# A four-layer image kernel on one core: some depthwise-convolution taps of the head moved from TensorE to VectorE

## The chip, the core and the metric

The kernel runs on one core of one Trainium2 chip. It uses TensorE for matrix products into PSUM (the memory that products accumulate in), VectorE, ScalarE and GpSimd for elementwise work, and SyncE to issue nearly all DMAs. In the profile these engines are PE (PEld for its weight loads), DVE, ACT, POOL and SP. [...] The metric is the device time of one execution in microseconds; a time given for a kernel is the median over several executions.

## The reference, cut to what matters

The input is four images of 96 channels and 64 x 64 pixels. Four layers are added to it in turn, each on a group-normalised copy of what came before.

```python
# layer 0: attention, plus a depthwise 5x5 convolution of v ("positional")
lepe = lax.conv_general_dilated(v, lepe_w, (1, 1), [(2, 2), (2, 2)], feature_group_count=C) + lepe_b
out = proj_w @ (feature + lepe) + proj_b
x = x + out
# layer 1: a state-space block; its input goes through a depthwise 3x3 convolution first
xz = jnp.einsum('bchw,oc->bohw', gn(x), in_proj_w)
xi, z = jnp.split(xz, 2, axis=1)                      # 192 channels each
xi = silu(conv2d(xi, conv_w, conv_b, groups=192, pad=1))
...                                                   # four directional scans over xi, then more convolutions
```

A depthwise convolution multiplies, for each channel, 25 (or 9) shifted copies of the image by one number each and adds them up. Layers 2 and 3 have convolutions and a second state-space block of the same kind.

## The kernel before, in words

**Stages.** `first(b)` computes layer 0 and the input half of layer 1 for image b; `second(b)` and `third(b)` the rest. The long recurrences of the two state-space blocks (the scans) are cut into 3072 units. The program has three parts. The head is `first(0)` alone, with `solo[0]` true. Then comes the scan part: 3072 calls of `unit`, with the stages of the other images laid beside them. Last comes the tail, `third` of the last image, again with `solo[0]` true. The scan part is emitted under a manual schedule, that is, in the order in which the program writes it. In the head the scheduler of the language orders the instructions of each engine.

**A convolution on TensorE.** Channels lie on the partitions. `diagonals` (from L1070) makes for each tap a 96 x 96 matrix that has that tap's 96 channel weights on its diagonal; `conv` (from L1083) multiplies it with the shifted window of a padded image and accumulates over the taps in one PSUM bank. One product covers 8 rows of 64 pixels, 512 columns; an image takes eight such chunks. In the profile one fp32 product shows as two matmul records.

**Positional convolution** (in `first`, from L1326). The padded image `vpad` is 68 x 68. For each of eight chunks j: 25 products into a bank, then VectorE adds the bank and the bias to `feat` (L1342), TensorE multiplies `feat` by the projection (l0_proj), VectorE adds that to `xn` (L1348), and the result is stored. After all eight, a group norm.

**Input convolution** (`in_conv`, from L1097). For each half h of 96 channels: eight products fill the padded image `upad` (66 x 66), copied in by ScalarE (L1107); then for each of eight chunks 9 products, a Silu from PSUM to `ur` by ScalarE (L1114), a transposed copy `uc` by ScalarE (L1115) and a store of `ur` (L1116). The transposed image is stored at the end of the half. `in_conv` is also called later, in `first` and `second` of other images, while scans run; there `solo[0]` is false.

**Banks in the head.** `bank()` with `solo[0]` true hands out halves of a two-bank tile `bx`, and two such tiles exist; so two convolutions share a tile, and the next two share the other. The waits follow the whole tile: the second convolution of a tile waits for the Silu that reads the first half.

**After the head.** `prepare(0)` makes the inputs of the first scan group from stored `ur` pieces (tile `us`, L1698): two small products per half, copies to `pr` (L1720), stores and loads, several ScalarE and GpSimd steps. Then `fetch`, `decays`, `drive`, `times_b` and the first `scan` (L1836) follow.

Of the kernel before, what the change touches and what calls it, by code (L numbers as in the profile page):

```python
# [9 lines left out]
F32 = mybir.dt.float32  # L10
BF16 = mybir.dt.bfloat16
AF = mybir.ActivationFunctionType
ALU = mybir.AluOpType
# [4 lines left out]
B, C, H, W = 4, 96, 64, 64  # L18
# [11 lines left out]
PCH = 512  # L30
# [162 lines left out]
def _view(t, slot, rows=None):  # L193
    n, m, shape = slot
    v = t[: rows or t.shape[0], n : n + m]
    if len(shape) == 1:
        return v
    names = "abcd"[: len(shape)]
    return v.rearrange(f"p ({' '.join(names)}) -> p {' '.join(names)}",
                       **{k: s for k, s in zip(names, shape)})  # L200
# [693 lines left out]
def streams(ctx: ExitStack, tc: tile.TileContext, x, wts, cst, out, wat, cat, flag):  # L894
# [3 lines left out]
    nc = tc.nc  # L898
# [16 lines left out]
    def wv(name, rows=None):  # L915
        return _view(wt, wat[name], rows)
# [27 lines left out]
    def img(t):  # L944
        return t.rearrange("p (a b) -> p a b", b=W)

    def mm(o, lhsT, rhs, first=True, last=True):
        nc.tensor.matmul(o, lhsT=lhsT, rhs=rhs, start=first, stop=last)  # L948

    solo = [True]  # L950
    spare = []

    def bank():
        if solo[0]:
            if not spare:
                t = ps.tile([128, CH], F32, tag="bx", name="bx")
                spare.extend((t[:, PCH:], t[:, :PCH]))
            return spare.pop()
        return ps.tile([128, PCH], F32, tag="one", name="one")
# [5 lines left out]
    def border(pad, k):  # L965
        n = pad.shape[1]
        for s in (pad[:, 0:k, :], pad[:, n - k : n, :], pad[:, k : n - k, 0:k], pad[:, k : n - k, n - k : n]):
            nc.gpsimd.memset(s, 0.0)
# [38 lines left out]
    with tc.tile_pool(name="start", bufs=1) as T:  # L1007
        t0 = T.tile([128, cst.shape[1] - n2], F32, name="t0")
        nc.scalar.dma_start(out=t0, in_=cst[:, n2:])
        n, m, shape = wat["l1_alog"]  # L1010
# [4 lines left out]
        n, m, shape = cat["spread"]  # L1015
        nc.vector.tensor_copy(spread, t0[:, n - n2 : n - n2 + m])
        for tag in ("l1_", "l3_"):
            decay[tag] = keep.tile([128, 4, E // 8], F32, name=tag + "decay")
            n, m, shape = cat[tag + "alogn"]
            src = _view(t0, (n - n2, m, shape))  # L1020
            if tag == "l3_":
                nc.scalar.activation(decay[tag], src, AF.Exp)
                src = decay[tag]
# [46 lines left out]
    def diagonals(pool, w, name="diag"):  # L1070

        taps = w.shape[1]
        w = w[:, :taps]
        d = pool.tile([96, taps, 96], F32, tag=name, name=name, bufs=1)
        nc.gpsimd.tensor_tensor(  # L1075
            d,
            ident[:96, :96].unsqueeze(1).to_broadcast([96, taps, 96]),
            w.unsqueeze(2).to_broadcast([96, taps, 96]),
            ALU.mult,
        )  # L1080
        return d

    def conv(o, weight, src, j, k=3):  # L1083


        n = k * k
        taps = [(weight[:, t, :], src[:, 8 * j + t // k : 8 * j + t // k + 8, t % k : t % k + W]) for t in range(n)]
        for t, (lhsT, rhs) in enumerate(taps):
            mm(o, lhsT, rhs, t == 0, t == len(taps) - 1)
            if t < len(taps) - 1:  # L1090
                yield (1,)
        yield

    def inner(pad, j):
        return pad[:, 1 + 8 * j : 9 + 8 * j, 1 : 1 + W]

    def in_conv(pool, tag, b, w, src):  # L1097

        pad = pool.tile([96, PADW, PADW], F32, name="upad", bufs=1)
        border(pad, 1)  # L1100
        for h in range(2):
            dg = diagonals(pool, wv(tag + "conv")[:, h, :])
            for j in range(8):
                p = bank()
                mm(p[:96], w[:, bass.ts(h, 96)], src[:, bass.ts(j, PCH)])
                yield
                nc.scalar.copy(inner(pad, j), img(p[:96]))  # L1107
                yield 1
            uc = pool.tile([96, W, H], F32, name="uc", bufs=1)
            for j in range(8):  # L1110
                p = bank()
                yield from conv(p[:96], dg, pad, j)
                ur = pool.tile([96, PCH], F32, name="ur", bufs=2)
                nc.scalar.activation(ur, p[:96], AF.Silu, bias=wv(tag + "conv_b")[:, h : h + 1])  # L1114
                nc.scalar.copy(uc[:, :, 8 * j : 8 * j + 8], ur.rearrange("p (a b) -> p b a", b=W))  # L1115
                nc.sync.dma_start(out=u_row[h][b][:, bass.ts(j, PCH)], in_=ur)  # L1116
                yield 1
            for j in range(4):
                nc.sync.dma_start(out=u_col[h][b][:, bass.ts(j, CH)],
                                  in_=uc.rearrange("p a b -> p (a b)")[:, bass.ts(j, CH)])  # L1120
# [179 lines left out]
    def first(b):  # L1300

        with tc.tile_pool(name="p1", bufs=1) as P:
            xn = P.tile([96, L], F32, name="xn")
            for j in range(4):
                nc.sync.dma_start(out=xn[:, bass.ts(j, CH)], in_=x[b][:, bass.ts(j, CH)])
            yield from group_norm(xn, img(xn))
            with tc.tile_pool(name="p1d", bufs=1) as D:
                samp = D.tile([96, 34, 34], F32, name="samp")
                dist = D.tile([96, 34, 34], F32, name="dist")
                for t in (samp, dist):  # L1310
                    border(t, 1)
                with tc.tile_pool(name="p1t", bufs=2) as T:
                    xv = xn.rearrange("p (i r j s) -> p i r j s", r=2, j=W // 2, s=2)
                    t0 = T.tile([96, 32, 32], F32, tag="t", name="t0")
                    t1 = T.tile([96, 32, 32], F32, tag="t", name="t1")
                    nc.vector.tensor_add(t0, xv[:, :, 0, :, 0], xv[:, :, 0, :, 1])
                    nc.vector.tensor_add(t1, xv[:, :, 1, :, 0], xv[:, :, 1, :, 1])
                    nc.vector.tensor_add(t0, t0, t1)
                    nc.vector.tensor_scalar(samp[:, 1:33, 1:33], t0, 0.25, None, ALU.mult)
                yield 2  # L1320
                yield from attention(b, xn, samp, dist)
                with tc.tile_pool(name="p1f", bufs=1) as FP:
                    feat = FP.tile([96, L], F32, name="feat")
                    yield from neighbours(b, xn, samp, dist, feat)
                    with tc.tile_pool(name="l0c", bufs=1) as pool:
                        w = staged(pool, "l0_v", "l0_proj")  # L1326
                        vpad = pool.tile([96, 68, 68], F32, name="vpad")
                        border(vpad, 2)
                        dg = diagonals(pool, wv("l0_lepe"))
                        for j in range(8):  # L1330
                            p = bank()
                            mm(p[:96], w["l0_v"], xn[:, bass.ts(j, PCH)])
                            yield
                            nc.scalar.copy(vpad[:, 2 + 8 * j : 10 + 8 * j, 2 : 2 + W], img(p[:96]))
                            yield 1
                        for j in range(4):
                            nc.sync.dma_start(out=xn[:, bass.ts(j, CH)], in_=x[b][:, bass.ts(j, CH)])
                        for j in range(8):
                            js = bass.ts(j, PCH)
                            p = bank()  # L1340
                            yield from conv(p[:96], dg, vpad, j, 5)
                            nc.vector.scalar_tensor_tensor(out=feat[:, js], in0=p[:96], scalar=wv("l0_lepe_b"),  # L1342
                                                           in1=feat[:, js], op0=ALU.add, op1=ALU.add)
                            yield 1
                            q = bank()
                            mm(q[:96], w["l0_proj"], feat[:, js])
                            yield
                            nc.vector.scalar_tensor_tensor(out=xn[:, js], in0=q[:96], scalar=wv("l0_proj_b"),  # L1348
                                                           in1=xn[:, js], op0=ALU.add, op1=ALU.add)
                            nc.sync.dma_start(out=res1[b][:, js], in_=xn[:, js])  # L1350
                            yield 1
            yield from group_norm(xn, img(xn))
            for j in range(4):
                nc.sync.dma_start(out=gate1[b][:, bass.ts(j, CH)], in_=xn[:, bass.ts(j, CH)])
            with tc.tile_pool(name="p1i", bufs=1) as pool:
                w = staged(pool, "l1_in")["l1_in"]
                yield from in_conv(pool, "l1_", b, w, xn)
# [615 lines left out]
    def beside(s):  # L1973
        stages = {"first": first, "second": second, "third": third}
        for n, b in BESIDE[s]:
            yield from stages[n](b)
# [50 lines left out]
    p = bank()  # L2027
# [36 lines left out]
```

## Time and profile before

| what | value |
|---|---|
| median of three executions | 15068.81 us (15060.3 to 15096.54) |
| the profiled execution, its own time | 15038.64 us |
| its span | 15036.8 us |
| busy over the span: PE, DVE, ACT, POOL | 82%, 78%, 55%, 69% |
| granted TensorE clock, mean | 0.809 |
| positional convolution of the head | 456 to 635 us |
| input convolution of the head | 642 to 786 us |
| first scan starts | 830.41 us |

How to read the profile: times are counted from the start of the span. A group's row gives the line, engine, operation, out<-in with shapes, its count, then busy time and the mean length of one, and then how long the engine sat idle just before and what released it. In a table by stretches each engine has its busy time and, in brackets, the number of instructions; behind them stand the granted TensorE clock (1.00 is full speed), the mean busy share of the 16 DMA engines, and GB/s. In a timeline a row gives start, length, engine, line, operation and count; in square brackets stands the idle time before it. The profiled execution is one of several, and it is 30 us below the median of the others.

### The profile page before, as it was taken

The page shows a single profiled execution, that of the slowest core. Times are in us where ns is not written, and L with a number is a line of the kernel's source. Part 1 is how long each engine was busy: PE and PEld are TensorE (multiplying, and loading weights), DVE is VectorE, ACT ScalarE, POOL GpSimd, SP SyncE. Part 2 cuts the span into 40 slices and gives each one's busy share as a digit, 9 for nine tenths or more (in the row PEclk, how much of TensorE's full clock was granted, in tenths as well). Part 3 has the DMA queues.
Part 4 walks back from the last instruction along what each step waited for, and adds up shares of the span by engine and source line. Part 5 has one row for each costly group of instructions (what it writes and reads, how often), then busy time and mean ns, then how long its engine had stood idle before and what let it go on. Part 6 is the DMA issues. An engine that isn't in the chain of part 4 may idle for free. (4 is left out here: it accounts for less than half of the span.)

```text
span 15036.8 us, 127166 instructions
## 1 busy us (share of the span) xinstructions
PE 12260.5 (82%) x40658; PEld 3344.2 (22%) x40658; DVE 11679.2 (78%) x7517; ACT 8280.8 (55%) x11648; POOL 10375.2 (69%) x4746
## 2 busy tenths in 40 slices
PE   8978886888969787889868887897969888667757
PEld 2322221222212222222212221221212222111111
DVE  0067888888878888778887798798878888777784
ACT  3155555555745566555655556455755567545652
POOL 0056787777868777668776787786777778666672
PEclk9978886898969888789867797797879888667666
DMA  0066788786878778667876788687877868666682
GB/s 9 26 149 163 177 202 213 175 211 171 215 178 203 195 183 209 167 168 197 208 179 158 170 204 222 174 203 180 203 195 192 203 173 221 168 166 167 167 204 68
DMA packets 902136, 2644.32 MB, mean 176 GB/s; under 512 B 107280, under 2 KB 257392, under 8 KB 901456
## 3 DMA queue, kind: packets, MB, share of 16 engines
q1 hardware_dynamic: 900800, 2634.83, 71.0%
q8 instruction: 323, 5.29, 0.2%
q14 instruction: 357, 2.92, 0.1%
q10 hardware_dynamic: 656, 1.27, 0.0%
HBM read 2169.08 MB, written 466.62 MB: 175 GB/s over the span
## 5 line engine op out<-in xcount | busy, mean ns | idle before, releaser
L1848 POOL TENSOR_TENSOR rep<-hs,bc 128x1024 f32<-128x1024 f32 x3072 | 7230.5, 2358 | 3160.0 <-DVE hs L1836 2682.5
L1836 DVE TENSOR_TENSOR_SCAN hs<-rep,carry,bx 128x1024 f32<-128x1024 f32 x2304 | 5401.4, 2344 | 277.9 <-POOL rep L1848 15.0
L1829 DVE TENSOR_TENSOR bx<-bx,bc 128x1024 f32<-128x1024 f32 x3072 | 3720.1, 1211 | 1033.6 <-PE bx L948 998.6
L1815 ACT ACTIVATE rep<-rep,l_decay 128x1024 f32<-128x1024 f32 x3072 | 3495.9, 1143 | 903.6 <-DMA rep<-dd 883.7
L948 PE MATMUL bx<-parts,spread 24*128 24x512 bf16 x6144 | 1413.5, 438 | 1812.0 <-DVE hs L1836 1762.5
L948 PE MATMUL acc<-rep,ct 128*32 128x512 f32 x12288 | 2603.0, 732 | 184.9 <-POOL rep L1848 184.9
L1836 DVE TENSOR_TENSOR_SCAN hs<-rep,bx 128x1024 f32<-128x1024 f32 x768 | 1754.2, 2284 | 306.9 <-POOL rep L1848 224.9
L948 PEld LDWEIGHTS <-spread 24*128 24x128 bf16 x6144 | 310.1, 93 | 4297.8 <-DVE hs L1836 2925.5
L948 PE MATMUL one<-band,dg 96*96 96x512 f32 x2304 | 1117.9, 621 | 0.0
L948 PE MATMUL one<-upad,diag 96*96 96x512 f32 x2016 | 1021.0, 643 | 3.2 <-ACT ur L1114 2.7
L948 PEld LDWEIGHTS acc<-rep,ct 128*32 128x32 f32 x12288 | 507.5, 126 | 1958.9 <-issue 1482.0
L948 PE MATMUL one<-qq,kk 96*128 96x512 f32 x1152 | 820.7, 802 | 133.8 <-ACT ex L1234 80.1
L1234 ACT ACTIVATE ex<-one 128x512 f32<-128x512 f32 x576 | 342.8, 595 | 754.1 <-PE one L948 749.3
L948 PE MATMUL one<-pr,ct 6*96 6x512 f32 x1024 | 647.1, 732 | 29.7 <-ACT pr L1720 4.1
L1815 ACT ACT_TABLE_LOAD x470 | 603.0, 1283 | 116.4 <-DMA rep<-dd 108.7
L948 PE MATMUL one<-hp,diag 96*96 96x512 f32 x1152 | 606.5, 665 | 48.0 <-POOL diag L1075 48.0
L948 PE MATMUL one<-vpad,diag 96*96 96x512 f32 x1200 | 590.7, 627 | 0.0
L1844 ACT COPY carry<-hs 128x1 f32<-128x1 f32 x2304 | 408.8, 177 | 314.4 <-DVE hs L1836 313.5
L948 PE MATMUL held<-ex,cols 128*32 128x256 f32 x3072 | 569.2, 451 | 12.0 <-ACT ex L1234 6.0
L948 PE MATMUL held<-ex,vT 128*32 128x256 f32 x3072 | 569.4, 451 | 0.0
L948 PEld LDWEIGHTS one<-band,dg 96*96 96x96 f32 x2304 | 350.6, 166 | 532.7 <-issue 517.1
L948 PEld LDWEIGHTS one<-upad,diag 96*96 96x96 f32 x2016 | 317.6, 172 | 490.0 <-issue 472.6
(3399 smaller groups left out, 13980.7 us busy)
## 6 DMA issues: line engine op xcount, KB each, us to landing
rep<-dd SPq DMA_DIRECT2D x3072, 512.0 KB
parts<-du SPq DMA_DIRECT2D x1024, 144.0 KB
bc<-rows SPq DMA_DIRECT2D x256, 512.0 KB
dd<-delta SPq DMA_DIRECT2D x256, 384.0 KB
du<-cut SPq DMA_DIRECT2D x256, 384.0 KB
us<-urow SPq DMA_DIRECT2D x128, 384.0 KB
du<-cut SPq DMA_DIRECT2D x256, 192.0 KB
yrow<-yo SPq DMA_DIRECT2D x128, 384.0 KB
```

Of the source, the lines that this page charges most:

```text
L948: nc.tensor.matmul(o, lhsT=lhsT, rhs=rhs, start=first, stop=last)
L1234: nc.scalar.activation(last.rearrange("p a b -> p (a b)"), p, AF.Exp, scale=HD**-0.5)
L1815: nc.scalar.activation(a, a, AF.Exp, scale=decay[tag][:, k, NG * h + m : NG * h + m + 1])
L1829: nc.vector.tensor_mul(bx, bx, ready[i // NG][2][:, 0, :])
L1836: nc.vector.tensor_tensor_scan(out=hs, data0=a, data1=bx, initial=carry[:, h, m : m + 1] if c else 0.0, op0=ALU.mult, op1=ALU.add)
L1844: nc.scalar.copy(carry[:, h, m : m + 1], live[i][1][:, CH - 1 : CH])
L1848: nc.gpsimd.tensor_tensor(a, hs, ready[i // NG][2][:, 1, :], ALU.mult)
```

## The change

Only where `solo[0]` is true, so in the head's two convolutions (the tail calls neither):

- Positional convolution: the first 11 of the 25 taps become 11 `scalar_tensor_tensor` instructions of VectorE per chunk, each `feat = window * weight + feat` in place. TensorE keeps 14 products per chunk.
- Input convolution: the first 4 of the 9 taps become, per chunk, one `tensor_scalar` and three `scalar_tensor_tensor` into a new tile `some` (two buffers), and one `tensor_add` that adds `some` to the bank in PSUM. The Silu then waits for that add. TensorE keeps 5 products per chunk.

The tap weights are read as one number per partition from the resident weight tile `wt`; the diagonal matrices are made as before.

```diff
+    def window(src, j, t, k):
+        return src[:, 8 * j + t // k : 8 * j + t // k + 8, t % k : t % k + W]
+
-    def conv(o, weight, src, j, k=3):
+    def conv(o, weight, src, j, k=3, first_=0):
...
-        taps = [(weight[:, t, :], src[:, 8 * j + t // k : 8 * j + t // k + 8, t % k : t % k + W]) for t in range(n)]
+        taps = [(weight[:, t, :], window(src, j, t, k)) for t in range(first_, n)]
...
                 p = bank()
-                yield from conv(p[:96], dg, pad, j)
+                if solo[0]:
+
+                    taken = wv(tag + "conv")[:, h, :]
+                    some = pool.tile([96, PCH], F32, name="some", bufs=2)
+                    nc.vector.tensor_scalar(img(some), window(pad, j, 0, 3), taken[:, 0:1], None, ALU.mult)
+                    for t in range(1, 4):
+                        nc.vector.scalar_tensor_tensor(out=img(some), in0=window(pad, j, t, 3),
+                                                       scalar=taken[:, t : t + 1], in1=img(some),
+                                                       op0=ALU.mult, op1=ALU.add)
+                yield from conv(p[:96], dg, pad, j, 3, 4 if solo[0] else 0)
+                if solo[0]:
+                    nc.vector.tensor_add(p[:96], p[:96], some)
...
                             p = bank()
-                            yield from conv(p[:96], dg, vpad, j, 5)
+                            if solo[0]:
+                                for t in range(11):
+                                    nc.vector.scalar_tensor_tensor(
+                                        out=img(feat[:, js]), in0=window(vpad, j, t, 5),
+                                        scalar=wv("l0_lepe")[:, t : t + 1], in1=img(feat[:, js]),
+                                        op0=ALU.mult, op1=ALU.add)
+                            yield from conv(p[:96], dg, vpad, j, 5, 11 if solo[0] else 0)
```

## The prediction

> **What bounds the kernel now.** I first read the page's busy shares: TensorE is busiest over the whole span, but that is a mean over the head, 14 ms of scans and a tail. The change touches only the head, so I read the table by stretches for its two convolutions and for the gap up to the first scan.
>
> ```profile
> 456.00:635.00 179.00, 179.00 (x415) 66.86 (x414) 15.29 (x21) 1.86 (x2) 0.00 (x0) 1.00 0.04 12
> 642.00:786.00 144.00, 144.00 (x327) 51.56 (x328) 2.06 (x3) 36.97 (x48) 1.63 (x1) 0.98 0.16 48
> 786.00:831.00 45.00, 7.13 (x14) 1.51 (x12) 3.02 (x4) 25.16 (x29) 11.24 (x5) 0.54 0.77 192
> ```
>
> Columns: length, then PE, PEld, DVE, ACT, POOL. In both convolutions TensorE has no idle time at full clock, VectorE works 15 of 179 us and 2 of 144 us, GpSimd hardly at all. What ends the idle time of the others, from the groups of 456 to 786 us, agrees:
>
> ```profile
> L948 PE MATMUL bx<-vpad,diag 96*96 96x512 f32 x400 | 174.3, 594 | 0.0
> L948 PE MATMUL bx<-upad,diag 96*96 96x512 f32 x288 | 125.3, 594 | 0.0
> L1115 ACT COPY uc<-ur 96x512 f32<-96x512 f32 x15 | 16.1, 1073 | 0.5
> L1114 ACT ACTIVATE ur<-bx,wt 96x512 f32<-96x512 f32 x16 | 10.9, 682 | 98.8 <-PE bx L948 98.8
> L1342 DVE SCALAR_TENSOR_TENSOR feat<-bx,wt,feat 96x512 f32<-96x512 f32 x8 | 6.0, 747 | 161.7 <-PE bx L948 161.7
> ```
>
> The Silu and the add of the positional result wait for the products, and no product waits. The price of a product comes from the timeline, since the 594 ns of a record overlap with the next:
>
> ```profile
> 456.14 23.55 PE L948 MATMUL bx<-vpad,diag 96*96 96x512 f32 x54
> 478.01 0.75 DVE L1342 SCALAR_TENSOR_TENSOR feat<-bx,wt,feat 96x512 f32<-96x512 f32 x1 [32.80 <-PE bx L948]
> 479.54 1.02 PE L948 MATMUL bx<-feat,l_proj 96*96 96x512 f32 x2
> 480.39 21.77 PE L948 MATMUL bx<-vpad,diag 96*96 96x512 f32 x50
> ```
>
> From 456.14 to 479.54 are 54 records, less about 0.3 us in which the projection was late; from 480.39 to the next projection at 502.01 are 50: 0.43 us a record, two records a product, so 0.857 us a product. Two products of the next chunk run before each projection and cover the add L1342.
>
> [...] The trace has no tap with both tensors in SBUF, but it has 1024 elements of two SBUF tensors at 1.22 us[...] here a dependent VectorE instruction starts about 0.1 us later than an independent one (below). [...]
>
> ```profile
> 22.09 2.98 DVE L1066 TENSOR_SCALAR xn<-xn,gn_g 96x1024 f32<-96x1024 f32 x4
> 25.10 1.22 DVE L1316 TENSOR_TENSOR t<-xn 96x1024 f32<-96x1024 f32 x1
> 26.24 1.22 DVE L1317 TENSOR_TENSOR t<-xn 96x1024 f32<-96x1024 f32 x1
> 27.49 1.22 DVE L1318 TENSOR_TENSOR t<-t,t 96x1024 f32<-96x1024 f32 x1
> 28.75 0.69 DVE L1319 TENSOR_SCALAR samp<-t 96x1024 f32<-96x1024 f32 x1
> ```
>
> L1317 does not need L1316 and starts 1.14 us after it; L1318 and L1319 need what precedes them and start 1.25 us later: length plus 0.03.
>
> **Removed.** Positional: 8 chunks x 11 products = 88, at 0.857 us 75.4 us. Input: 16 chunks x 4 = 64, 54.8 us. Together 130.2 us, all of it on the path, since TensorE has no gap there. The diagonal matrices stay and are off the path.
>
> **Added in the positional stage.** 88 taps on VectorE. The nearest row is a scalar_tensor_tensor with a per-partition weight, 0.747 us (L1342, one operand in PSUM). Bounds for start to start: [...] 0.78 (0.747 + 0.03, each waiting for the one before). In the instruction order of the built change the taps of two chunks are partly woven together; I take 0.74. Per chunk 11 x 0.74 + 0.75 + 0.78 + 0.69 for the statistics = 10.4 us, below TensorE's 15 x 0.857 = 12.9. But the built order puts taps well ahead of need: 27 taps before the first L1342, then 18, 17 and 18 taps between the next ones, and only 8 after these. In those three intervals VectorE needs 18 x 0.74 + 0.75 + 0.78 = 14.9 us against 12.9, and the projection, which needs L1342, holds up TensorE. By hand: taps can start when the first `vpad` chunk is copied (449.1), 27 of them end at 469.1, L1342 at 469.9; TensorE has finished chunk 0 and two products of chunk 1 at 469.9: no loss. The following three lose 1.9, 1.2 and 2.0 us; from chunk 4 VectorE is ahead again. Loss 5 us; with 0.70 it is 2.4, with 0.78 8.3[...]. The stage then takes 120 x 0.857 + 5 = 108 us of VectorE 88 x 0.74 + 17 = 82 busy.
>
> **Added in the input stage.** Per chunk: a tensor_scalar of 512 elements (half of L1066's stream: about 0.42 us), three taps at 0.78 and an add in PSUM of 0.68 (L1139, the same form, 681 ns): 3.5 us of VectorE against 5 x 0.857 = 4.29 of TensorE, and 1.75 of ScalarE (0.68 + 1.07). The new wait stands in the chain: products, add, Silu, then the second convolution of the tile. From the end of a convolution that is 0.1 + 0.68 + 0.05 + 0.68 + 0.1 = 1.6 us; behind the waiting add on VectorE stand the taps of the next chunks, which TensorE doesn't need until their own add. The built order gives TensorE three leftover products of one convolution and two of the next tile between, 4.3 us in which both tiles' waits end; I find a stall of about 0.8 us at the first pair, 0.2 for each of the six others and 0.5 where the halves change: 2.5 us. With the add one tap late (0.78 us a pair) it is 8. At the end, one add more before the last Silu, 0.8 us; against that two `pr` copies (0.58 each) now stand ahead of it on ScalarE and the loads of `bc` ahead of the last stores on SP: about 0.5 us gained. SP's queue has no new entries; the 6.3 MB of `ur` and `uc` stores now go out in some 85 us instead of 134, about 75 GB/s, where the stretch after the head carries 192. Stores land before their buffer is wanted again: a piece every 4.3 us, two buffers.
>
> **Passing on.** The first scan at 830.41 follows from the last convolution by a chain of dependent steps of 45 us, with no DMA in it that was issued before the head's end, so it moves as a whole. The order in the scan part is the same program. Sum: 130.2 - 5 - 2.5 - 0.5 = 122 us. Against the profiled execution 15038.6 - 122 = 14916.6; against the median, which lies 30 above it, 15068.8 - 122 = 14947.
>
> **Rivals.** *VectorE becomes the bound.* For it: in 45 us of scans the same engine shows 1.2 to 2.8 us on windowed operands (L1317 has a mean of 2823 ns over four calls, 1.22 in the head). Against: GpSimd is idle in both stretches. If a tap took 1.1 us: positional 88 x 1.1 + 17 + 2 = 116 us, saving 63; input (0.42 + 3.3 + 0.75) x 16 = 72 + 14 for the `upad` products = 86 against 144, saving 55 less some stalls, 45. Gain 108 at most, 90 with front loading: 14979.
> *TensorE's clock drops, slower.* The place is the two convolutions, whose products now stop for 1 to 2 us. For it: at 430 to 450 us TensorE is busy 8 to 9 of 10 us at clock 0.50 to 0.57, a product of 8 rows 1.70 us. At that clock the 216 products left take 367 us, with stalls 374, against 323 before: 15120. It decides from a mean clock under 216 x 0.857 / (185 + 122) = 0.60. Against: 50 to 100 us has 44.4 of 50 busy with waits of 0.7 to 0.9 us, clock 1.00.
> *Lost later.* The scan part takes up the gain (loads of the first group bind instead). Then nothing measurable changes: 15069. Against: every such load is issued after the head's last products.
>
> **Numbers.** Forecast, gain 110 to 130: 0.83. VectorE bound, gain 50 to 110: 0.10. Lost later: 0.03. Clock: 0.03. Larger gain through the reordered end: 0.01. What can be told from no change is 0.3%, 45 us; the first, second and last lie beyond it: faster 0.94, same 0.03, slower 0.03. The range: gain 130 to 95 gives 14939 to 14974; the executions of before scatter by -9 and +28 around their median, and the profiled one by -30; so 14910 to 14985.
>
> **What would show it.** Positional stretch of 105 to 112 us, TensorE's idle there before the projections of chunks 1 to 3 and released by `feat`; taps at 0.70 to 0.78; input stretch of 88 to 95 us with Silu released by VectorE; gap to the first scan 45 us; clock 1.00 in both stretches. A stretch length near VectorE's busy time, or a clock under 0.9, would prove it wrong.

## The result, and the profile after

| | before | after |
|---|---|---|
| median | 15064.56 us (15033.04 to 15096.54, 4 executions) | 14916.25 us (14908.91 to 14939.95, 4 executions) |
| ratio to before | | 0.9904, 95% interval 0.9890 to 0.9918 |
| span of the profiled execution | 15036.8 us | 14907.1 us |
| positional stage | 185.9 us | 109.7 us |
| input stage | 143.6 us | 91.6 us |
| gap to the first scan | 44.8 us | 43.7 us |
| first scan to the end of the span | 14206.4 us | 14205.5 us |

The kernel before has one execution more here (15033.04 us) than ahead of the prediction. The positional stage is counted from its first product on `vpad` to the first l_in product; so it holds the group norm at its end as well, some 6 us that the prediction's stretch (456 to 635 us) left out. The input stage runs from there to the end of the last product on `upad`, the gap from there to the first scan. The three together are 374.3 us before and 245.0 after: 129.3 us less, which is the difference of the two spans (129.7) but for 0.4. The changed kernel's table of these three stretches, with the columns as before (length, PE, PEld, DVE, ACT, POOL, clock, DMA share, GB/s):

```profile
456.67:566.34 109.67, 104.87 (x245) 39.12 (x245) 71.17 (x111) 2.13 (x3) 2.00 (x5) 0.99 0.08 23
566.34:658.00 91.66, 90.24 (x202) 30.90 (x204) 54.01 (x82) 37.78 (x49) 1.63 (x1) 0.97 0.26 77
658.00:701.70 43.70, 6.19 (x12) 1.09 (x12) 3.18 (x5) 24.31 (x27) 11.25 (x5) 0.53 0.73 188
```

TensorE still fills both stages, at nearly full clock; its 4.8 idle us in the positional stage lie behind the last product, at the last projection and the group norm, and were 4.8 before as well. VectorE's busy time went from 19 to 71 us and from 2 to 54. The groups of the changed kernel from 456 to 660 us show who waits for whom now:

```profile
L948 PE MATMUL bx<-vpad,diag 96*96 96x512 f32 x224 | 98.2, 594 | 0.0
L948 PE MATMUL bx<-upad,diag 96*96 96x512 f32 x160 | 70.7, 596 | 1.4 <-ACT ur L1128 1.4
L1357 DVE SCALAR_TENSOR_TENSOR feat<-vpad,wt,feat 96x512 f32<-96x512 f32 x81 | 54.6, 743 | 0.0
...
L1126 DVE TENSOR_TENSOR bx<-bx,some 96x512 f32<-96x512 f32 x16 | 11.1, 693 | 31.7 <-PE bx L948 31.7
L1128 ACT ACTIVATE ur<-bx,wt 96x512 f32<-96x512 f32 x16 | 10.9, 684 | 46.0 <-DVE bx L1126 46.0
L1110 ACT COPY upad<-bx 96x512 f32<-96x512 f32 x16 | 9.3, 582 | 9.3 <-PE bx L948 9.3
L948 PE MATMUL bx<-feat,l_proj 96*96 96x512 f32 x16 | 8.2, 596 | 0.8 <-DVE feat L1362 0.8
```

The Silu (L1128, once L1114) is now released by VectorE's add, and the add by TensorE. The projection waits for `feat` only 0.8 us, once, at the last chunk. The timeline of the positional stage, VectorE first and then TensorE, shows why:

```profile
449.74 2.33 DVE L1357 SCALAR_TENSOR_TENSOR feat<-vpad,wt,feat 96x512 f32<-96x512 f32 x3 [3.94 <-ACT vpad L1348]
453.01 15.99 DVE L1357 SCALAR_TENSOR_TENSOR feat<-vpad,wt,feat 96x512 f32<-96x512 f32 x24 [0.94 <-ACT vpad L1348]
469.03 0.75 DVE L1362 SCALAR_TENSOR_TENSOR feat<-bx,wt,feat 96x512 f32<-96x512 f32 x1
...
482.28 0.74 DVE L1362 SCALAR_TENSOR_TENSOR feat<-bx,wt,feat 96x512 f32<-96x512 f32 x1
```

```profile
470.57 1.02 PE L948 MATMUL bx<-feat,l_proj 96*96 96x512 f32 x2
471.43 12.27 PE L948 MATMUL bx<-vpad,diag 96*96 96x512 f32 x28
483.54 1.02 PE L948 MATMUL bx<-feat,l_proj 96*96 96x512 f32 x2
484.40 12.28 PE L948 MATMUL bx<-vpad,diag 96*96 96x512 f32 x28
```

The projections stand 12.97 us apart, 15 products of 0.865 us, with no bracket of idle time. VectorE's 24 woven taps take 15.99 us, 0.66 us each from start to start. The first two adds L1362 come 13.25 us apart, so VectorE is 0.3 us slower than TensorE here, but each add ends before TensorE is through with its two products in hand.

### The profile page after: what moved, and what is told of

It is laid out like the page before. It is cut to its first block, busy times and chain, and to the rows that moved or that the text cites. A ratio compares the mean times of both kernels' runs of the same rounds, so it can differ in the third digit from the quotient of the medians.

```text
span 14907.1 us, 126739 instructions
## 1 busy us (share of the span) xinstructions
PE 12122.0 (81%) x40354; PEld 3289.6 (22%) x40354; DVE 11789.6 (79%) x7685; ACT 8282.7 (56%) x11648; POOL 10381.2 (70%) x4746
## 5 line engine op out<-in xcount | busy, mean ns | idle before, releaser
L1856 DVE TENSOR_TENSOR_SCAN hs<-rep,carry,bx 128x1024 f32<-128x1024 f32 x2304 | 5401.0, 2344 | 277.1 <-POOL rep L1868 13.7
```

Source lines behind the costliest of these rows:

```text
L1856: nc.vector.tensor_tensor_scan(out=hs, data0=a, data1=bx, initial=carry[:, h, m : m + 1] if c else 0.0, op0=ALU.mult, op1=ALU.add)
```

## The experiments

For each kernel the same three stretches are read from its timeline:

| kernel | positional | input | gap | sum | first scan to end |
|---|---|---|---|---|---|
| before | 185.9 | 143.6 | 44.8 | 374.3 | 14206.4 |
| changed | 109.7 | 91.6 | 43.7 | 245.0 | 14205.5 |
| e1 positional only | 109.7 | 144.1 | 44.3 | 298.0 | 14248.1 |
| e2 input only | 186.0 | 90.9 | 44.5 | 321.4 | 14254.9 |
| e3 taps left out | 109.8 | 88.9 | 45.7 | 244.4 | 14246.7 |
| e4 taps and all products | 185.8 | 144.3 | 43.8 | 373.9 | 14257.4 |
| e5 13 positional taps | 95.8 | 91.6 | 44.1 | 231.5 | 14228.8 |
| e6 13, chained | 103.0 | 91.3 | 43.6 | 237.9 | 14202.6 |
| e7 17 positional taps | 109.6 | 91.8 | 43.7 | 245.1 | 14248.3 |
| e8 5 input taps | 109.8 | 86.6 | 42.9 | 239.3 | 14255.0 |
| e9 13 and 5 taps | 95.9 | 85.1 | 42.8 | 223.8 | 14236.1 |
| e0 changed again | 109.8 | 91.3 | 43.7 | 244.8 | 14236.1 |

The theory under test: each stage is as long as TensorE's queue plus its waits, VectorE's work hides beside it while its queue is the shorter one, and all that follows moves as a whole.

### One part alone

```diff
 # e1: the input convolution as before
-                yield from conv(p[:96], dg, pad, j, 3, 4 if solo[0] else 0)
+                yield from conv(p[:96], dg, pad, j, 3, 0)
 # e2: the positional convolution as before
-                            yield from conv(p[:96], dg, vpad, j, 5, 11 if solo[0] else 0)
+                            yield from conv(p[:96], dg, vpad, j, 5, 0 if solo[0] else 0)
```

(with the VectorE instructions of that part taken out)

> Only the positional taps on VectorE; the input convolution keeps its 9 products per chunk. Stage lengths: positional from its first vpad product to the first l_in product (before 185.9 us, changed 109.7), input from there to the last upad product's end (143.6 and 91.5), gap from there to the first scan (44.8 and 43.8). Theory (each stage is as long as TensorE's queue plus its waits, and the rest moves as a whole): 109.7, 143.6, 44.8; first scan near 755 us, 76 us earlier than before; whole execution 76 us shorter than before. Rival (the scan part gave some of the gain, or the two parts help each other): the two single parts don't add up to the 129 us by which the first scan moved, or the stretch from the first scan to the end is not the 14206 us of both kernels.

> Only the input taps on VectorE; the positional convolution keeps 25 products per chunk. Theory: positional 185.9, input 91.5, gap 43.8; first scan near 778 us, 53 earlier than before. Rival (the parts don't add up): more than 3 us off any of these, or the first scan to the end differs from 14206 by more than 10.

The three stretches came out 76.3 and 52.9 us shorter than before, together 129.2 against 129.3 for both parts in one kernel. The whole executions: 14984.55 us against 15057.61 (ratio 0.9945, interval 0.9928 to 0.9961) and 14991.93 (0.9949, 0.9932 to 0.9965), both within reach of 76 and 53 us (the quotients of the medians themselves are 0.9952 and 0.9956). What did not fit is the rest of the program: from the first scan to the end it took 14248 and 14255 us, 42 to 49 more than in the two kernels profiled first. By the letter of the expectation that speaks for the rival, so it needed a reading of its own; it follows under "The scan part".

### VectorE's work without its relief, and the relief without the work

```diff
 # e3: products left out, no VectorE taps
-                                for t in range(11):
+                                for t in range(0):
...
 # e4: taps on VectorE, and all products on TensorE too
-                            yield from conv(p[:96], dg, vpad, j, 5, 11 if solo[0] else 0)
+                            yield from conv(p[:96], dg, vpad, j, 5, 0 if solo[0] else 0)
```

(and the same for the input taps; e3 leaves the add in PSUM out too, so its convolutions lack those taps)

> The 11 and 4 taps are left out of both convolutions altogether: TensorE has the products of the changed kernel, VectorE and the add in PSUM have nothing of it. It measures what the VectorE work itself costs. Theory (hidden in the positional stage, exposed in the input stage through the add and the tile's wait): positional 109.7 within 1 us, input 2 to 4 us shorter than 91.5. Rival (taps laid ahead hold up the projections, the 5 us of the prediction): positional 103 to 105 us.

> VectorE does its taps and TensorE keeps all 25 and 9 products as well, so the taken taps count twice. Theory (VectorE's work is free while TensorE is the longer queue, and costs no clock and no SBUF bandwidth of the products): positional 185.9, input 143.6 to 147, clock 1.00, first scan 830 to 834, whole execution within 0.3% of before. Rival (two engines reading the padded image, or a fuller VectorE, slow the products or the clock): products above 0.43 us a record, positional over 188 us.

Without the taps the positional stage is 109.8 us, with them 109.7: 88 taps cost nothing there, and the 5 us of the prediction don't exist. The input stage is 88.9 us without and 91.6 with them, so the add and the tile's wait cost 2.7 us; the gap is 2.0 us longer without, so 0.6 us net remains. With the taps and all products, everything is as before: 185.8 and 144.3 us, ratio to before 1.0004 (0.9993 to 1.0015). The groups of that kernel, e4:

```profile
L948 PE MATMUL bx<-vpad,diag 96*96 96x512 f32 x400 | 174.3, 594 | 0.0
L948 PE MATMUL bx<-upad,diag 96*96 96x512 f32 x288 | 124.9, 593 | 0.5 <-ACT ur L1128 0.5
...
L1121 DVE SCALAR_TENSOR_TENSOR some<-upad,wt,some 96x512 f32<-96x512 f32 x48 | 35.6, 747 | 1.6
```

The product records have the length that they had before (594 ns), though both engines read the padded image. VectorE's work costs nothing here beside the longer queue.

### How far it goes

```diff
 # e5: 13 taps (e7: 17)
-                                for t in range(11):
+                                for t in range(13):
-                            yield from conv(p[:96], dg, vpad, j, 5, 11 if solo[0] else 0)
+                            yield from conv(p[:96], dg, vpad, j, 5, 13 if solo[0] else 0)
 # e6: 13 taps that accumulate in one buffer
+                                held_ = pool.tile([96, PCH], F32, name="held_", bufs=1)
...
-                                        out=img(feat[:, js]), in0=window(vpad, j, t, 5),
+                                        out=img(held_), in0=window(vpad, j, t, 5),
...
 # e8: 5 input taps
-                    for t in range(1, 4):
+                    for t in range(1, 5):
...
```

> 13 instead of 11 positional taps on VectorE, 12 products per chunk on TensorE; the input convolution as in the changed kernel. From the measured prices (a tap 0.66 us where it lies between taps of another chunk, a product 0.857): VectorE needs 13 x 0.66 + 0.66 + 0.67 + 0.6 = 10.5 us per chunk against 13 x 0.857 = 11.1 on TensorE, so TensorE still bounds: positional 109.7 - 16 x 0.857 = 96.0 us, at most 98 with the taps that are laid ahead; first scan 13.7 us earlier, whole execution 0.9% to 1.1% below the one before the change. Rival (VectorE bound is already reached, at the chained price 0.79): positional 101 to 105 us.

> 13 positional taps that accumulate in one single buffer, so that the taps of a chunk can't be woven with those of the next and each waits for the one just before it; same count of instructions as e5, nothing laid ahead. Theory (a dependent tap costs 0.79, and only then does VectorE bind): taps at 0.79 start to start, VectorE 13 x 0.79 + 2.0 = 12.3 us per chunk against 11.1, positional 102 to 106 us, TensorE idle before each projection, released by feat. Rival (the length of a tap, not what stands before it, sets its price): positional as in e5, 96 to 98.

> 17 positional taps on VectorE, 8 products per chunk on TensorE, woven as the scheduler lays them. Theory (VectorE is now the longer queue): 17 x 0.66 + 1.93 = 13.2 us per chunk against 9 x 0.857 = 7.7: positional 103 to 110 us, no better than with 11. Rival (only the number of products counts): 109.7 - 48 x 0.857 = 68.6 us.

> 5 instead of 4 input taps on VectorE, 4 products per chunk on TensorE; the positional convolution as in the changed kernel. Theory (VectorE and the add become the longer loop): per chunk 0.5 + 4 x 0.70 + 0.65 = 3.95 us against 4 x 0.857 = 3.43; input stage 84 to 90 us where products alone would give 91.5 - 13.7 = 77.8, with the Silu and TensorE waiting for the add in each pair. Rival (products alone count): 77 to 79.

With 13 taps the positional stage is 95.8 us, the 13.9 us of 16 more products gone; the whole execution took 14911.26 us against 15071.35 (0.9895, 0.9878 to 0.9913). With the same 13 taps in one buffer it is 103.0. (e6, e7 and e8 were executed once each, so of them only the stages are read: e6's 14897.04 us lie below e5's median although its head is 6.4 us longer.) VectorE's timeline of the chained kernel, e6, and then of e5:

```profile
449.13 9.43 DVE L1358 SCALAR_TENSOR_TENSOR held__2075<-vpad,wt,held__2075 96x512 f32<-96x512 f32 x12
...
477.52 0.75 DVE L1364 SCALAR_TENSOR_TENSOR feat<-bx,wt,held__2106 96x512 f32<-96x512 f32 x1
...
489.57 0.75 DVE L1364 SCALAR_TENSOR_TENSOR feat<-bx,wt,held__2137 96x512 f32<-96x512 f32 x1
```

```profile
452.02 14.00 DVE L1357 SCALAR_TENSOR_TENSOR feat<-vpad,wt,feat 96x512 f32<-96x512 f32 x21 [0.79 <-ACT vpad L1348]
...
477.57 0.74 DVE L1362 SCALAR_TENSOR_TENSOR feat<-bx,wt,feat 96x512 f32<-96x512 f32 x1
...
488.82 0.74 DVE L1362 SCALAR_TENSOR_TENSOR feat<-bx,wt,feat 96x512 f32<-96x512 f32 x1
```

A tap behind its own result starts 0.79 us after it (9.43 us for 12); woven with taps of another chunk 0.66 (14.00 for 21). Each one is 0.74 to 0.75 us long in both. The profile doesn't say to which chunk a tap belongs; that they are woven is read from the order of instructions. What ties the price to the dependence is that both prices stand in one kernel: the changed kernel's first three taps, ahead of the next wait for `vpad`, take 2.33 us, 0.79 apart, and in e6 a tap that stands behind an instruction that it doesn't read starts 0.66 us after it (L1370 at 468.50, the tap at 469.16). The adds then come 12.05 us apart against 11.25. TensorE works ahead as long as it can, and in e6 the projections wait for `feat` 6.1 us in all, 4.9 of them before the last one.

With 17 taps the stage is as long as with 11. The table of e7 from 456 to 566 us, and three projections of its timeline:

```profile
456.00:566.00 110.00, 78.82 (x150) 26.86 (x150) 102.34 (x159) 2.17 (x4) 2.00 (x5) 0.78 0.08 23
```

```profile
472.34 1.86 PE L948 MATMUL bx<-feat,l_proj 96*96 96x512 f32 x2 [2.11 <-DVE feat L1362]
...
499.57 2.02 PE L948 MATMUL bx<-feat,l_proj 96*96 96x512 f32 x2 [7.49 <-DVE feat L1362]
...
527.32 2.02 PE L948 MATMUL bx<-feat,l_proj 96*96 96x512 f32 x2 [5.63 <-DVE feat L1362]
```

VectorE is busy 102 of 110 us, so the stage is as long as its queue. TensorE waits for it up to 7.5 us at a time, and its clock falls to 0.78 of full: a projection behind a wait takes 1.86 to 2.02 us instead of 1.02. Two rivals of the prediction are real at 17 taps and absent at 11; what the lower clock costs beside the waits was not separated.

With 5 input taps the stage is 86.6 us: shorter than with 4, but by 5.0 us where 16 products less are 13.7. The expectation gave VectorE's longer loop as the reason, with a wait in each pair; the number fits it, but the trace doesn't. The table of the stage, for e8 and then the changed kernel, and two pieces of TensorE's timeline of each:

```profile
567.00:654.00 87.00, 84.11 (x172) 27.80 (x174) 65.01 (x100) 40.73 (x53) 1.63 (x1) 0.89 0.30 87
566.00:658.00 92.00, 90.24 (x202) 30.93 (x204) 54.35 (x83) 37.78 (x49) 1.63 (x1) 0.97 0.26 77
```

```profile
588.94 17.50 PE L948 MATMUL bx<-upad,diag 96*96 96x512 f32 x32 [1.88 <-ACT ur L1128]
...
646.73 7.07 PE L948 MATMUL bx<-upad,diag 96*96 96x512 f32 x8
```

```profile
589.86 17.63 PE L948 MATMUL bx<-upad,diag 96*96 96x512 f32 x40 [0.72 <-ACT ur L1128]
...
653.40 4.53 PE L948 MATMUL bx<-upad,diag 96*96 96x512 f32 x10 [0.71 <-ACT ur L1128]
```

TensorE is idle for 2.7 us of e8's stage (1.88 and 0.80), against 1.4 in the changed kernel (0.72 and 0.71); only the first pair waits for the Silu behind the add, 1.88 us. But behind that wait 32 records take as long as 40 do in the changed kernel, and the last eight take 7.07 us where ten take 4.53. At the changed kernel's pace the two pieces would be 3.5 and 3.4 us shorter: in each, eight records run at about half speed. The weight loads of the first piece show it: behind the wait they come 0.85 us apart from 589.90 to 595.02 us, and 0.43 apart from 595.75 on. The granted clock agrees: 0.89 over e8's stage against 0.97, as the two rows of the table show. With the 1.3 us of longer waits that is 8.2 of the missing 8.7 us. So most of what 5 taps fail to gain is a lower clock. In the first piece it follows a single wait; what set off the second was not tried.

### The best of both, and the changed kernel again

```diff
+                                for t in range(13):
+                    for t in range(1, 5):
 # conv(..., vpad, j, 5, 13 ...) and conv(..., pad, j, 3, 5 ...)
```

> 13 positional and 5 input taps on VectorE, the two settings that shortened their stage most, in one kernel. Theory (the stages add up): positional 95.8 us as with 13 taps, input 86.6 as with 5, gap 43 to 44; from the first vpad product to the first scan 225.8 us, 19 less than the changed kernel's 245.0 and 148.5 less than before's 374.3; ratio to the kernel before 0.988 to 0.990. Rival (the two settings share something, so that they don't add up): over 230 us.

> The changed kernel once more, on the same chip and beside the same runs of before as the one with 13 and 5 taps. Theory: from the first vpad product to the first scan 245.0 us; ratio to before 0.989 to 0.993 (129 us of 15060 is 0.9914), so that the 141 to 148 us between the medians of the first runs are the 129 of the head and scatter of the scan part. Rival (part of the gain comes from the scan part): the head's 129 again, but a ratio whose interval lies below 0.9905.

The settings add up, to within 2 us: 223.8 us from the first product to the first scan, 21.2 less than the changed kernel, where 225.8 was expected. The input stage gives 1.5 of these 2 us; its last eight records take 5.37 us here, not 7.07 as in e8. Over the whole execution e9 took 14897.8 us and the changed kernel 14929.17, beside 15044.71 for the one before: ratios 0.9891 (0.9873 to 0.9909) and 0.9905 (0.9888 to 0.9923). Each is faster than before, by about 1%, with an interval that lies below 1; their intervals overlap, so the step from 11 and 4 to 13 and 5 taps is shown by the stages and not by the total time. The changed kernel's interval holds the 0.9914 that 129 us alone would give, and 0.9905 is no lower than its first ratio, so nothing speaks for a gain in the scan part.

### The scan part

The table of the stretch from the first scan to the end, for the kernel before, the changed one and e4:

```profile
830.40:15036.00 14205.60, 11521.86 (x37630) 3075.15 (x37630) 11607.89 (x7400) 8062.07 (x11290) 10343.15 (x4703) 0.80 0.75 185
```

```profile
701.70:14907.00 14205.30, 11514.21 (x37630) 3070.59 (x37630) 11607.87 (x7400) 8063.89 (x11290) 10349.05 (x4703) 0.80 0.75 185
```

```profile
829.60:15087.00 14257.40, 11572.53 (x37630) 3087.20 (x37630) 11604.53 (x7400) 8065.67 (x11290) 10343.34 (x4703) 0.80 0.75 184
```

The counts of instructions are the same to the last one, and VectorE, ScalarE and GpSimd are busy the same within 6 us. TensorE alone is busy 51 to 58 us longer in e4, and that stretch is 52 us longer. In e4 the head is as long as before and the whole execution too (1.0004), so this is scatter of an unchanged part from one execution to the next, not a product of the change; the executions of the kernel before spread over 80 us by themselves. The plainest sign is e0: the changed kernel itself, unaltered, took 14236.1 us in this stretch the second time, 31 more than the first. e1 and e2 are read in the same way: TensorE's busy time in their scan parts is 11578 and 11564 us, the other engines' as here; their heads carry the change, their scan parts the scatter. That TensorE's busy time goes with it is what these lines show. The granted clock of whole executions goes with it too: of the twelve of e4 the shortest, 15022.69 us, had a mean of 0.813 and the longest, 15103.01, one of 0.804. Why the clock is lower in some executions was not tried and stays open.

## Why the prediction was right

**The path.** That both stages were as long as TensorE's queue, and that each product taken away is worth its full price, held: 88 products gave 76.2 us (75.4 forecast), and e1 and e5 repeat it (76.2 for 88, 13.9 for 16, 0.87 us each against 0.857). The prediction's own lines give the larger price: the 50 records in the 21.62 us from 480.39 to 502.01 are 0.865 us a product. In its first interval nothing was late, since products run on up to the projection, so the 0.3 us should not have been taken off: 23.40 us for 54 records are 0.867. For the input stage e3 gives 54.7 us for the 64 products, as forecast (54.8).

**The VectorE taps.** The step that was mis-sized. The prediction took 0.74 us a tap, the author's estimate, a little below the 0.78 of a tap that waits for the one before, and from that and the taps laid ahead a loss of 5 us; its own calculation said 2.4 us at 0.70. Measured: 0.66 woven, 0.79 chained, and no loss. The order was as forecast, 18 taps between the first two adds; but they took 13.25 us with the two instructions beside them, not 14.9, against TensorE's 12.97, and the slack of the first chunk covered the 0.3 us. So of its signs the idle time before the projections of chunks 1 to 3 never showed, and the taps lay below 0.70 to 0.78. The 109.7 us of the table are not its "105 to 112" come true either: counted as it counted, from the first to the last product on `vpad`, the stage went from 179.1 to 103.1 us, below that range. The instruction order had shown that the taps are woven, and the trace of before had the price of an independent neighbour, its length of 1.22 us less 0.08 (from L1316 to L1317 1.14); 0.747 - 0.08 = 0.67 could have been read there.

**The add and the tile's wait.** Forecast as 2.5 us of stalls; e3 shows 2.7, in part by luck. The tensor_scalar was 0.48 us instead of 0.42, the add 0.69 instead of 0.68; but in the changed kernel TensorE's bracketed waits for the Silu are two, of 0.7 us each, at the first pair and before the last convolution. The 0.2 us at each of six other pairs are not to be seen, and 1.3 of the 2.7 us are not traced to a place.

**The end of the head.** Forecast: 0.8 us lost, 0.5 gained (its sum then took 0.5 off, not 0.3). The gap became 1.1 us shorter; it varies by that much between kernels of the same order there (43.7 to 44.8), so no more can be read from it.

**Passing on.** The gap and the scan part moved as a whole, as forecast. The sum was 122 us and the stretches give 129; of the missing 7, 5 are the loss that never came, 0.8 the price of the positional products and 1.6 the end of the head, less 0.3 in the input stage. The median fell by 148 us at first and by 115 us in the last comparison (15044.71 - 14929.17), on both sides of 129. That the first median lies inside the range of 14910 to 14985 is therefore in part luck: a fall of 148 us is beyond the forecast gain of 110 to 130, and the allowance for scatter took it in. The head's 129 us lie inside that gain, near its upper end.

**The rivals.** "VectorE becomes the bound" was wrong at 11 taps and right at 17, and its price of 1.1 us a tap appears nowhere. That an idle GpSimd speaks against it was the author's estimate and was not tested. The rival's sum has a slip that changes nothing: 144 less 86 is 58 us, not 55. "TensorE's clock drops" was wrong here, 0.99 and 0.97 over the two stages, but with little to spare: with one input tap more, products at half speed followed a wait of 1.88 us (e8), where the clock stayed at 1.00 behind two waits of 0.7 us in the changed kernel. In the kernel before, a wait of 2.54 us stands ahead of the 8-row products at 430.92 us, and the clock is 0.57 from 430 to 440 us and 0.50 from 440 to 450. "Lost later" falls with the unchanged scan part.

## What to carry to other kernels

Where one engine fills a stage and another is nearly idle, move work until both queues are nearly equally long per loop turn, counting the prices that the trace shows for that neighbourhood; of the 11, 13 and 17 positional taps tried, 13 were best. Leave enough slack that the first engine's waits stay short: in e8 the slow products behind one wait of 1.88 us took 3.5 us more. Count a stage by its own stretch: a gain of 20 us in a head is plain there (the changed kernel's stages came out within 0.3 us of each other in two executions) and lost in the scatter of 14 ms behind it. Lay dependent VectorE instructions of two independent chains in turn; here that made 0.66 us a tap out of 0.79.

## What the runs showed of the hardware that was not expected

The start-to-start time of the same 512-element scalar_tensor_tensor was 0.79 us when it read what the instruction just before it wrote, and 0.66 us between instructions of another chain, less than its own length of 0.74: such neighbours overlapped by 0.08 us. In e8 VectorE's loop is by the expectation's estimate longer than TensorE's (3.95 us against 3.43), and yet TensorE was busy for 83.9 of the stage's 86.6 us: what was lost shows as slower products and hardly as waiting. Busy time alone would have hidden it; the length of like groups of records, side by side, shows it.
